# An RWKV block on one core: own sums in the decay product's fourth column tile, a first mix input from PSUM, and a new order

## The chip, the core and the metric

The kernel runs on one core of one Trainium2 chip. The core's engines are TensorE (PE in the profile, with PEld for its weight loads), VectorE (DVE), ScalarE (ACT), GpSimd (POOL) and SyncE (SP, which here only issues loads and stores). The metric is the device time of one execution in microseconds; the time of a version is the median of its runs. Lower is better.

## What is computed

One block of a recurrent network (RWKV) on `x` of shape 8 x 256 x 512 in float32: a normalisation, a mix of each token with the one before it (the token shift), five mixed inputs, a recurrence over the 256 tokens with a 16 x 16 state in each of 32 heads, a normalisation of each head, an output product, and then a second, simpler half. Cut to what matters here:

```python
xn = _ln(x, ln1_w, ln1_b)
sx = _token_shift(xn, state[:, i1])            # previous token minus this one
xxx = jnp.tanh((xn + sx * maa_x) @ maa_w1)     # 5 groups of 32
xxx = jnp.matmul(xxx, maa_w2)
x5 = xn[:, :, None] + sx[:, :, None] * (maa_stack + xxx)
w = jnp.exp(-jnp.exp(time_decay + jnp.tanh(x5[:, :, 1] @ decay_w1) @ decay_w2))
r, k, v = x5[3] @ Wr.T, x5[0] @ Wk.T, x5[2] @ Wv.T
g = silu(x5[4] @ Wg.T)
def step(s, rkvw):                              # over the tokens
    a = k_t[:, :, :, None] * v_t[:, :, None, :]
    out = jnp.einsum('bhk,bhkd->bhd', r_t, u * a + s)
    return (a + w_t[:, :, :, None] * s, out)
x = x + (head_norm(outs) * gn_w + gn_b) * g @ Wo.T
x = x + sigmoid(xr @ ffn_Wr.T) * (square(relu(xk @ ffn_Wk.T)) @ ffn_Wv.T)
```

The term with `u` in a step's output doesn't need the state: it is `v_t` times the sum over a head's 16 channels of `r * u * k`. The kernel computes that sum apart; this document calls it the **own sum** (a token's own part).

## The kernel before, in words

A batch (256 tokens) goes through three stages: `inputs_of_scan` (normalise, mix, the four projections k, v, r, g and the decay w), `scan` (the recurrence) and `rest` (head norm, output product, second half). Stages of neighbouring batches overlap. A class `Plan` collects the pieces of work of every stage, each with its engine, its buffers and a duration. `order` then places them one after another: the numbers in the table `TURNS` are the ranks of the pieces, and the piece of the lowest rank that has its inputs is placed next. The outcome is a fixed instruction order for each engine; each engine works its own list strictly in order.

Arrays lie with channels on the 128 partitions, four blocks of 128 channels in two pairs (q = 0, 1; m = 0, 1 within a pair). TensorE multiplies float32 (two records in the trace for a matmul), either with the whole 128 x 128 array, with four column tiles of 32 side by side ("columns", L400 with 128*32, L794, L872, L930), or with row tiles. PSUM, which TensorE writes, has six tiles `ps` of 2 x 256 columns and one wide tile `wrep`.

The scan of a batch runs in four blocks of 128 channels. For each block come four loads `vs` (v spread over the partitions), on VectorE a multiply by k (L917) and a scan along the tokens (L919, `st`), on GpSimd a multiply by r (L922), and on TensorE the block sum of the four products (L930, 16 matmuls); L936 adds it to `att`. Some of the multiplies by k in the first two batches are GpSimd's (L914).

`att` holds v times the own sum. Before the change `scan` makes it: GpSimd multiplies r by k (L867, `rk`), TensorE sums it over the heads with the head masks `hm`, four matmuls in four column tiles (L872), ScalarE copies the result to `att` in 16 pieces of 32 partitions x 256 (L880), GpSimd multiplies by v (L886).

The decay w takes two small products. The first (L794, "the decay product" below) uses four column tiles at once: two for the 64 columns of `decay_w1` on x5[1], and two for the fifth group of `maa_w1` on the first mix input `xin`, which gives `tb` (L802). That group has only 32 columns; both tiles compute it, so that rows 96 to 127 repeat rows 64 to 95. The second (`w,dw`) follows tanh.

At the launch, batch 0's normalised x is turned by TensorE (L612). Then VectorE makes xn from PSUM (L626, times `ln1_w` plus `ln1_b`), ScalarE makes xn * (1 - maa_x) from it into PSUM (L629, the factor `ow` from L529), and VectorE adds the previous token times maa_x (L655): the first mix input. ScalarE then takes tanh of its product with `maa_w1` (L713, `ta`), TensorE multiplies by `maa_w2` (w2a), and VectorE forms x5 (L748, L751). The head masks `hm` are four small VectorE instructions (L533). The parameter vectors `vec` come by SyncE's queue, the identity `idt` by ScalarE's. Wv is centred on the core: TensorE multiplies it by a matrix, and ScalarE copies the four results (L515).

## Time and profile before

| | |
|---|---|
| median of 3 runs | 609.45 us (609.26 to 609.94) |
| span of the profiled execution, first to last instruction | 607.3 us |
| lies around the span, median less span | 2.15 us |
| TensorE busy | 597.2 us |
| VectorE, ScalarE, GpSimd busy | 543.9, 514.6, 520.2 us |
| TensorE clock granted | 1.000 |
| read from and written to memory | 115.25 and 8.39 MB |

The page gives the span as the profiled execution's own time; what lies around it is known only from the median. A row of a group gives line, engine, operation, output <- inputs, shapes and count, then the busy time and the mean of one in ns, then the idle time ahead of it and what ended it. A row of a timeline gives the start, the length, the engine, the line, the operation and the count; neighbours of one kind are merged. A busy TensorE means only that a matmul was in flight.

### The profile page before, as it was taken

To read this page: it belongs to the slowest core of one execution; us is meant where nothing else is said; L and a number is where in the kernel's file an instruction comes from. 1 tells how busy PE (TensorE), PEld (TensorE's weight loads), DVE (VectorE), ACT (ScalarE), POOL (GpSimd) and SP (SyncE) were. 2 spreads that over 40 slices of the span, in tenths; PEclk is the share of its full clock that TensorE was granted. 3 is DMA by queue.
4 is the path that set the end of the run, shared out by engine and by line. 5 is a ranking of instruction groups with operands and counts; after the bars stand their busy time and mean duration, and the time that the engine had idled before them with its cause. 6 is when DMAs were issued, how large, how long until landed. Compare 5 with 4: busy or idle time off the path is not lost.

```text
span 607.3 us, 17606 instructions
## 1 busy us (share of the span) xinstructions
PE 597.2 (98%) x7270; PEld 344.8 (57%) x7270; DVE 543.9 (90%) x492; ACT 514.6 (85%) x1172; POOL 520.2 (86%) x417
## 2 busy tenths in 40 slices
PE   9999999999999999999999999999999999999997
PEld 7675555467544664377553775455644464446464
DVE  6699999999999998899989999999999999995442
ACT  6878779999999999999999898999989799965450
POOL 2899999999899999899989998999898998898020
PEclk9999999999999999999999999999999999999999
DMA  8798855878778787859767996688659877951542
GB/s 319 224 266 218 232 147 142 227 181 215 220 220 215 219 219 205 213 145 268 198 198 191 277 239 189 186 240 225 188 174 263 203 204 227 258 186 42 175 168 92
DMA packets 52640, 124.77 MB, mean 205 GB/s; under 512 B 5841, under 2 KB 11345, under 8 KB 52561
## 3 DMA queue, kind: packets, MB, share of 16 engines
q1 hardware_dynamic: 48048, 119.39, 71.3%
q10 hardware_dynamic: 4512, 4.26, 2.3%
q8 instruction: 57, 0.93, 0.7%
q14 instruction: 23, 0.18, 0.1%
HBM read 115.25 MB, written 8.39 MB: 204 GB/s over the span
## 4 chain that ended last, share of the span: by engine, by line
PE 78%; POOL 14%; DVE 3%; issue 3%; ACT 1%; DMA 1%; DVEq 0%; POOLq 0%; ACTq 0%
PE ps L400 65%; PE ps L930 8%; POOL st L922 7%; PE ps L612 2%; POOL mix L754 2%; PE ps L794 2%; POOL vs L914 2%; DVE st L919 1%; POOL mix L782 1%; POOL att L886 1%; POOL sx L640 1%; PE ps L956 1%; DMA xt<-in_x 1%; PE ps L872 0%; DVE vs L917 0%
## 5 line engine op out<-in xcount | busy, mean ns | idle before, releaser
L919 DVE TENSOR_TENSOR_SCAN st<-wrep,vs 128x1024 f32<-128x1024 f32 x128 | 288.2, 2277 | 2.9 <-ACT wrep L900 0.8
L922 POOL TENSOR_TENSOR st<-st,r 128x1024 f32<-128x1024 f32 x128 | 254.5, 2005 | 9.3 <-DVE st L919 9.0
L917 DVE TENSOR_TENSOR vs<-vs,ps 128x1024 f32<-128x1024 f32 x122 | 143.7, 1208 | 2.6 <-ACT vs L910 2.4
L400 PE MATMUL ps<-Ws,mix 128*32 128x512 f32 (+3 forms) x872 | 115.2, 586 | 0.1
L400 PEld LDWEIGHTS ps<-Ws,mix 128*32 128x32 f32 (+1 forms) x872 | 37.6, 116 | 63.4 <-issue 56.0
L754 POOL TENSOR_TENSOR mix<-mix,xn 128x512 f32<-128x512 f32 x62 | 66.6, 1098 | 6.9 <-DVE mix L738 5.5
L930 PE MATMUL ps<-st,con 128*32 128x256 f32 x1024 | 62.1, 380 | 0.8 <-POOL st L922 0.7
L400 PE MATMUL ps<-mix,Wv 128*32 128x256 f32 (+1 forms) x832 | 60.5, 380 | 1.6 <-DVE mix L751 0.9
L400 PE MATMUL ps<-mix,Wk 128*32 128x256 f32 (+1 forms) x952 | 59.2, 379 | 0.1
L400 PE MATMUL ps<-mix,Wg 128*32 128x256 f32 (+1 forms) x664 | 58.8, 379 | 0.0
L400 PE MATMUL ps<-mix,Wr 128*32 128x256 f32 (+1 forms) x688 | 58.5, 380 | 0.0
L400 PE MATMUL ps<-mix,Ws 128*32 128x256 f32 (+1 forms) x664 | 57.3, 379 | 0.0
L400 PE MATMUL ps<-Ws,g 128*32 128x512 f32 (+1 forms) x416 | 56.9, 593 | 0.2 <-POOL g L1001 0.2
L736 ACT ACTIVATE ps<-ps,vec 128x256 f32<-128x256 f32 x112 | 47.6, 444 | 3.8 <-PE ps L400 2.3
L880 ACT COPY att<-ps 32x256 f32<-32x256 f32 x128 | 46.6, 364 | 4.4 <-ACT v L825 1.3
L668 POOL TENSOR_TENSOR mix<-mix,xn 128x512 f32<-128x512 f32 x44 | 47.3, 1093 | 3.4 <-ACT mix L666 3.2
L400 PEld LDWEIGHTS ps<-mix,Wv 128*32 128x32 f32 (+1 forms) x832 | 37.7, 116 | 21.2 <-DVE mix L751 1.6
L400 PEld LDWEIGHTS ps<-mix,Ws 128*32 128x32 f32 (+1 forms) x664 | 40.0, 124 | 15.5 <-ACT o L1025 0.5
L400 PEld LDWEIGHTS ps<-mix,Wr 128*32 128x32 f32 (+1 forms) x688 | 39.3, 123 | 16.5 <-issue 1.3
L930 PEld LDWEIGHTS ps<-st,con 128*32 128x32 f32 x1024 | 32.7, 110 | 27.5 <-issue 4.4
L400 PEld LDWEIGHTS ps<-mix,Wg 128*32 128x32 f32 (+1 forms) x664 | 39.9, 124 | 14.8 <-issue 0.7
L400 PEld LDWEIGHTS ps<-mix,Wk 128*32 128x32 f32 (+1 forms) x952 | 35.0, 112 | 22.3 <-issue 2.9
(141 smaller groups left out, 968.1 us busy)
## 6 DMA issues: line engine op xcount, KB each, us to landing
vs<-vo SPq DMA_DIRECT2D x128, 512.0 KB, 5.7
Ws<-in_fk SPq DMA_DIRECT2D x16, 512.0 KB, 6.1
Ws<-in_wo SPq DMA_DIRECT2D x16, 512.0 KB, 6.2
Ws<-in_fr SPq DMA_DIRECT2D x16, 512.0 KB, 6.1
Ws<-in_fv SPq DMA_DIRECT2D x16, 512.0 KB, 5.2
x<-in_x SPq DMA_DIRECT2D x9, 512.0 KB, 8.0
vo<-v ACTq DMA_DIRECT2D x15, 256.0 KB, 5.4
out<-o SPq DMA_DIRECT2D x15, 256.0 KB, 4.9
```

The source lines that it names most:

```text
L400: nc.tensor.matmul(out[i : i + n], lhsT=w[:, i : i + n], rhs=x, start=first, stop=final)
L612: nc.tensor.transpose(to[:, m, n * P : (n + 1) * P], xh[n]()[:, k * P : (k + 1) * P], idt())
L668: gp(512, t, [t, xn[q]], lambda q=q, t=t: nc.gpsimd.tensor_tensor(t(), t(), xn[q]()[:, :, 1 : T + 1], ALU.add))
L736: act(256, p_, [p_, vec], lambda g=g, q=q, m=m, p_=p_: nc.scalar.activation(p_()[:, m, :], p_()[:, m, :], AF.Identity, bias=col(f"maa_{g}" ...
L754: gp(512, t, [t, xn[q]], lambda q=q, t=t: nc.gpsimd.tensor_tensor(t(), t(), xn[q]()[:, :, 1 : T + 1], ALU.add))
L794: nc.tensor.matmul(pd()[i : i + 32, 0, :], lhsT=w, rhs=src[k // 2]()[:, k % 2, :], start=(k == begin), stop=(k == end))
L880: act(350, atts[q], [pc], lambda i=32 * (2 * q + m), m=m, q=q, h=32 * h: nc.scalar.copy(atts[q]()[h : h + 32, m, :], pc()[i : i + 32, 0, :]))
L914: gp(4 * T, vs, [vs, k], lambda m=m, vs=vs, k=k: nc.gpsimd.tensor_tensor(vs(), vs(), k.place[:, m : m + 1, 1 : T + 1].to_broadcast([P, 4, ...
L917: dve(4 * T, [vs], [vs, kp], lambda m=m, vs=vs, kp=kp: nc.vector.tensor_tensor(vs(), vs(), kp()[:, m : m + 1, :].to_broadcast([P, 4, T]), ...
L919: dve(4 * T, [st], [w, vs], lambda w=w, vs=vs, st=st: nc.vector.tensor_tensor_scan(st().rearrange("p n t -> p (n t)"), w().rearrange("p n ...
L922: gp(4 * T, st, [st, r], lambda m=m, st=st, r=r: nc.gpsimd.tensor_tensor(st(), st(), r()[:, m : m + 1, :].to_broadcast([P, 4, T]), ALU.mul ...
L930: nc.tensor.matmul(pat()[32 * i : 32 * i + 32, 0, :], lhsT=con()[:, s : s + 32], rhs=done[i]()[:, j, :], start=(j == 0), stop=(j == 3),)
```

## The change

The own sums of batches 0 to 6 move into the decay product of the next batch: its fourth column tile, rows 96 to 127, no longer repeats the `maa_w1` columns but multiplies one block of `rk` by `hm`. Their results lie in two PSUM tiles, the decay product's own `pd` and one more. `tb` is therefore written in four pieces of 32 partitions, not in two of 64. ScalarE copies the sums to `att` in eight pieces of 32 x 512. Batch 7 keeps the old form. The multiplies `rk` move from `scan` to the end of `inputs_of_scan`, and the stages are put down in a new sequence, with the inputs of batch b + 1 ahead of the scan of b.

At the launch the first mix input comes straight from PSUM: ScalarE makes `xn * (1 - maa_x)` from PSUM with combined factors `ow` and bias `ln1_b`, VectorE adds the previous token from PSUM times `xw`, and the first column has a one-element instruction of its own with `xb`. `ow`, `xw` and `xb` take six small GpSimd instructions in place of one. Of the four centred Wv pieces VectorE copies two. `vec` is loaded by ScalarE's queue. `TURNS` is new throughout.

```diff
+        if b == NB - 1: ...   (batch 7: product and 16 copies as before)
+        else:
+            for q, pc in enumerate(got["pc"]):
+                for h in range(0, P, 32):
+                    act(610, atts[q], [pc], lambda q=q, h=h, pc=pc: nc.scalar.copy(atts[q]()[h : h + 32], pc()[96:128]))
...
-                    for i in range(0, P, 32):
+                    for i in range(0, P if b == 0 else 96, 32):
                         w, src = (dw1()[:, k, i : i + 32], x5[1]) if i < DEC else (w1()[:, k, P + i - DEC : P + i - 32], xin)
                         nc.tensor.matmul(
                             pd()[i : i + 32, 0, :], lhsT=w, rhs=src[k // 2]()[:, k % 2, :], start=(k == begin), stop=(k == end))
+                    if own:
+                        nc.tensor.matmul(own["pc"][k // 2]()[96:128, k % 2, :], lhsT=hm()[:, k, :],
+                                         rhs=own["rks"][k // 2]()[:, k % 2, :], start=True, stop=True)
...
-        for rows in (slice(0, 64), slice(64, 128)):
-            act(T, tb, [pd], lambda rows=rows: nc.scalar.activation(tb()[rows, :], pd()[64:128, 0, :], AF.Tanh), "exp")
+        n = 32 if own else 64
+        for rows in (slice(i, i + n) for i in range(0, P, n)):
+            act(T, tb, [pd], lambda rows=rows: nc.scalar.activation(tb()[rows, :], pd()[64 : 64 + n, 0, :], AF.Tanh), "exp")
...
                 if first:
+                    t = first[q]
+                    a = new(("sq", "o")[m], f"xa_{q}_{m}")
+                    act(256, a, [ps, ow, vec], lambda m=m, k=k, a=a, ps=ps: nc.scalar.activation(
+                        a()[:, 0:T], ps()[:, m, :], AF.Identity, bias=col("ln1_b", k), scale=ow()[:, k : k + 1]), pointers=2)
+                    dve(1, [t], [ps, ow, xb], lambda m=m, k=k, t=t, ps=ps: nc.vector.tensor_scalar(
+                        t()[:, m, 0:1], ps()[:, m, 0:1], ow()[:, k : k + 1], xb()[:, k : k + 1], ALU.mult, ALU.add))
+                    dve(256, [t], [ps, a, xw], lambda m=m, k=k, t=t, a=a, ps=ps: nc.vector.scalar_tensor_tensor(
+                        t()[:, m, 1:T], ps()[:, m, 0 : T - 1], xw()[:, k : k + 1], a()[:, 1:T], ALU.mult, ALU.add), 1.28)
                     dve(256, [xn], [ps, vec], lambda m=m, k=k, xn=xn, ps=ps: nc.vector.tensor_scalar(
                         xn()[:, m, 1 : T + 1], ps()[:, m, :], col("ln1_w", k), col("ln1_b", k), ALU.mult, ALU.add))
-                    t = ps
-                    act(256, t, [xn, ow], lambda m=m, k=k, t=t, xn=xn: nc.scalar.activation(
-                        t()[:, m, :], xn()[:, m, 1 : T + 1], AF.Copy, scale=ow()[:, k : k + 1]), pointers=1)
...
-            act(512, w, [ps], lambda ps=ps, w=w: nc.scalar.copy(w(), ps().rearrange("p m t -> p (m t)")))
+            if k % 2:
+                act(512, w, [ps], lambda ps=ps, w=w: nc.scalar.copy(w(), ps().rearrange("p m t -> p (m t)")))
+            else:
+                dve(512, [w], [ps], lambda ps=ps, w=w: nc.vector.tensor_copy(w(), ps().rearrange("p m t -> p (m t)")))
...
+    plan.add("ACT", 0.4, [vec], [], lambda: nc.scalar.dma_start(out=vec(), in_=vecs), kb=64)
-    load(vec, vecs, 64)
...
     TURNS = """
-        1 69 8 22 53 86 91 104 59 88 92 103 194 171 11 27 85 123 124 180 9 7 10 38 39 63 31 52 68 37 41 44 46 47 48,
+        5 3 49 10 30 35 34 85 67 56 71 61 76 39 4 18 23 13 14 15 25 103 115 118 121 8 7 9 38 62 68 48 72 82 52
```

What this moves is seen in the instruction lists. In them the lines are those of the changed kernel where it is the changed kernel's list (L794 is now L812, the own sums stand at L815, L930 is L962, L533 is L556, L748 and L751 are L766 and L769, L713 is L731). A row gives the line, the operation, output <- inputs with the numbers of the buffers, and the shape of the output.

TensorE before, at batch 0's own sums (about 53 us): two projections' last rows, the own sums of batch 0 by themselves, and the block sum.

```order
L400 MATMUL ps_170<-mix_113,Wg_81 32x256 x8
L400 MATMUL ps_174<-mix_108,Wg_80 32x256 x8
L400 MATMUL ps_174<-mix_113,Wg_81 32x256 x8
L872 MATMUL ps_173<-rk_151,hm 32x256 x2
L872 MATMUL ps_173<-rk_152,hm 32x256 x2
L930 MATMUL ps_171<-st_156,con 32x256
L930 MATMUL ps_171<-st_154,con 32x256
```

TensorE in the changed kernel at the same place: batch 1's decay product with batch 0's own sums in it, between the g projection and the block sum.

```order
L410 MATMUL ps_176<-mix_115,Wg_83 32x256 x8
L812 MATMUL ps_175<-mix_114,dw_69 32x256 x2
L812 MATMUL ps_175<-mix_111,mw_66 32x256
L815 MATMUL ps_175<-rk_153,hm 32x256
L812 MATMUL ps_175<-mix_114,dw_69 32x256 x2
L812 MATMUL ps_175<-mix_111,mw_66 32x256
L815 MATMUL ps_175<-rk_153,hm 32x256
L812 MATMUL ps_175<-mix_113,dw_69 32x256 x2
L812 MATMUL ps_175<-mix_109,mw_66 32x256
L815 MATMUL ps_173<-rk_154,hm 32x256
L962 MATMUL ps_176<-st_158,con 32x256
```

The four separate matmuls are gone; in each group of four column tiles the second copy of `mw` has become a matmul on `rk`, and the decay product, which before came after this block sum, now comes ahead of it.

VectorE before, at the launch between batch 1's statistics and the third x5 input (`mix_111` and `mix_115` are the second and last pieces of x5[2], from which Wv is multiplied).

```order
L574 BN_STATS st_89<-x_161 128x6
L575 BN_AGGR mv_92<-st_89 128x2
L748 SCALAR_TENSOR_TENSOR ps_170<-ps_170,vec,sx_103 128x256 x2
L751 TENSOR_TENSOR mix_111<-ps_170,xn_99 128x512
L748 SCALAR_TENSOR_TENSOR ps_172<-ps_172,vec,sx_104 128x256 x2
L751 TENSOR_TENSOR mix_115<-ps_172,xn_100 128x512
L533 TENSOR_SCALAR hm<-con,vec 128x32
```

VectorE in the changed kernel, the same stretch from the last piece of the first mix input on (`mix_113` and `mix_117` are the pieces of x5[2]).

```order
L651 SCALAR_TENSOR_TENSOR mix_110<-ps_172,xw,o_166 128x255
L528 COPY Wv_79<-ps_177 128x512
L528 COPY Wv_78<-ps_174 128x512
L653 TENSOR_SCALAR xn_102<-ps_172,vec 128x256 x2
L595 BN_STATS st_92<-x_163 128x6
L595 BN_STATS st_91<-x_163 128x6
L596 BN_AGGR mv_94<-st_92 128x2
L596 BN_AGGR mv_94<-st_91 128x2
...
L769 TENSOR_TENSOR mix_113<-ps_174,xn_101 128x512
L766 SCALAR_TENSOR_TENSOR ps_176<-ps_176,vec,sx_106 128x256 x2
L556 TENSOR_SCALAR hm<-con,vec 128x32
L769 TENSOR_TENSOR mix_117<-ps_176,xn_102 128x512
```

Two Wv copies and two xn pieces now stand ahead of the statistics, and a head mask stands ahead of the last addition, where before it came behind it.

ScalarE before, at the very start.

```order
L1058 DMA idt<-in_consts 128x128
L462 ACT_TABLE_LOAD
L462 ACTIVATE mn_94<-eh 128x2
L565 ACTIVATE rs_95<-mv_91,eh 128x1
L565 ACTIVATE rs_96<-mv_92,eh 128x1
```

ScalarE in the changed kernel, at the very start.

```order
L1091 DMA vec<-in_vecs 128x128
L472 ACT_TABLE_LOAD
L472 ACTIVATE mn_96<-eh 128x2
L1090 DMA idt<-in_consts 128x128
L586 ACTIVATE rs_97<-mv_93,eh 128x1
```

The vectors take the identity's place at the head of the queue; the identity is issued behind the table load and the first activation.

77 lines of the change are left out of this document (42 added, 35 removed), and 246 rows, old and new, of the table TURNS.

## The prediction

> **What bounds the kernel now.** I read the page first: the busy time of each engine, then the chain that ended last.
>
> ```profile
> PE 597.2 (98%) x7270; PEld 344.8 (57%) x7270; DVE 543.9 (90%) x492; ACT 514.6 (85%) x1172; POOL 520.2 (86%) x417
> PE 78%; POOL 14%; DVE 3%; issue 3%; ACT 1%; DMA 1%; DVEq 0%; POOLq 0%; ACTq 0%
> ```
>
> TensorE (PE) is busy for 98% of the span and carries 78% of the chain, so work taken from it should shorten the kernel. But GpSimd (POOL) carries 14%, and an average does not say where. The busy times by stretch (columns: length, then PE, PEld, DVE, ACT, POOL) and the chain in order of time do.
>
> ```profile
> 50.00:75.00 25.00, 25.00 (x464) 14.78 (x458) 25.00 (x22) 20.09 (x47) 25.00 (x18) 1.00 0.89 222
> 450.00:500.00 50.00, 50.00 (x724) 26.63 (x720) 48.26 (x43) 44.06 (x100) 46.49 (x36) 1.00 0.83 218
> ...
> 34.21 2.00 POOL st L922
> ...
> 140.21 1.97 POOL st L922
> 142.22 1.93 PE ps L930 x32
> ```
>
> Between 50 and 75 us GpSimd and VectorE never rest either; between 450 and 500 only TensorE is always busy. The chain hangs mostly on GpSimd's multiplies from 34 us up to the block sum at 142 us (L930, TensorE's sum over the four products of one block), and from there on TensorE. TensorE's own timeline has the wait at that point:
>
> ```profile
> 142.22 1.93 PE L930 MATMUL ps<-st,con 128*32 128x256 f32 x32 [0.33 <-POOL st L922]
> ```
>
> So there are three stages: a launch, in which each engine waits for another; a GpSimd stage up to 142 us, in which TensorE work is free; and a TensorE stage, in which it is the price. The sum is made against the span of 607.3; the median of the runs, 609.45, lies 2.15 above it, and I keep that.
>
> **The change, part by part. The own sums.** Seven of the eight products at L872 vanish as work of their own: they go into the fourth column tile of the decay product (L794), which until now computed rows 64 to 95 a second time in rows 96 to 127.
>
> ```profile
> 182.66 0.61 PE L872 MATMUL ps<-rk,hm 128*32 128x256 f32 x8
> 183.09 1.91 PE L400 MATMUL ps<-mix,Wv 128*32 128x256 f32 x32
> ...
> busy tenths in 40 slices 0002002000002020000200000200002000200000
> L872 PE MATMUL ps<-rk,hm x64: 379/379/403, 52.9 to 523.5; 128*32 128x256 f32 x64
> L794 PE MATMUL ps<-mix,mw x128: 379/379/403, 19.3 to 484.2; 128*32 128x256 f32 x128
> ```
>
> One of them costs 183.09 - 182.66 = 0.43 us of TensorE, start to start. The new instructions have the shape of those that they replace (L872 and L794 both 379 ns, the same tile), so the fourth column costs nothing more. The marks of L872 in 40 slices of 15.2 us are at slices 3, 6, 12, 14, 19, 25, 30 and 34: the first two lie before 142 us, where TensorE has time to spare, and the last one, batch 7's, stays. What counts is **5 x 0.43 = 2.15 us off**. If the two early ones counted as well it would be 3.0.
>
> ScalarE copies the sums out in another form:
>
> ```profile
> L880 ACT COPY att<-ps 32x256 f32<-32x256 f32 x128 | 46.6, 364 | 4.4 <-ACT v L825 1.3 <-PE ps L872 1.3
> L825 ACT COPY k<-ps 128x512 f32<-128x512 f32 x16 | 9.3, 581 | 3.1 <-PE ps L400 3.0
> L802 ACT ACTIVATE tb<-ps 64x256 f32<-64x256 f32 x16 | 6.1, 381 | 0.7 <-ACT v L843 0.4
> ```
>
> Sixteen copies at 0.364 are 5.8 us a batch; eight copies of twice the columns, by the nearest row 0.58 each, are 4.6; two more tanh pieces at 0.38 add 0.8. That is 0.4 us less ScalarE work a batch, 2.8 in seven. ScalarE stands on 1% of the chain, so of the bounds, nothing and 2.8 off, I take nothing; TensorE's own work hides it. The products r*k move ahead on GpSimd, sixteen before and after, nothing.
>
> **The launch.** The rows of VectorE, TensorE, ScalarE and GpSimd, by engine:
>
> ```profile
> 7.15 1.00 DVE L626 TENSOR_SCALAR xn<-ps,vec 128x256 f32<-128x256 f32 x2 [0.53 <-PE ps L612]
> 9.39 1.66 DVE L655 SCALAR_TENSOR_TENSOR mix<-xn,vec,ps 128x256 f32<-128x256 f32 x4
> 11.12 0.69 DVE L574 BATCH_NORM_STATS2 st<-x 128x6 f32<-128x512 f32 x1
> 14.35 1.02 DVE L748 SCALAR_TENSOR_TENSOR ps<-ps,vec,sx 128x256 f32<-128x256 f32 x2 [1.51 <-PE ps L400]
> 16.01 1.01 DVE L748 SCALAR_TENSOR_TENSOR ps<-ps,vec,sx 128x256 f32<-128x256 f32 x2
> 17.05 0.69 DVE L751 TENSOR_TENSOR mix<-ps,xn 128x512 f32<-128x512 f32 x1
> 17.66 1.17 DVE L533 TENSOR_SCALAR hm<-con,vec 128x32 f32<-128x32 f32 x1
> ...
> 17.53 1.27 POOL L744 TENSOR_TENSOR mix<-mix,sx 128x512 f32<-128x512 f32 x1
> ...
> 10.52 1.94 PE L400 MATMUL ps<-mix,mw 128*128 128x256 f32 x8
> 17.80 1.13 PE L400 MATMUL ps<-mix,Wv 128*128 128x256 f32 x4
> 26.61 0.71 PE L400 MATMUL ps<-tb,mw2b 32*128 32x256 f32 x8
> ...
> 12.62 0.38 ACT L713 ACTIVATE ta<-ps 128x256 f32<-128x256 f32 x1
> ...
> L567 DVE RECIPROCAL rs<-rs 128x1 f32<-128x1 f32 x2 | 0.3, 155 | 0.0
> ```
>
> Before, VectorE makes four xn pieces and four mix pieces, and the first mix input stands at 9.39 + 1.66 = 11.05. Now only two xn pieces lie ahead: 2 x 0.50, four one-column pieces (at 0.155, the nearest short row) 0.6, and 1.66, from 7.15 to 10.4: 0.65 earlier. TensorE's first product then ends near 12.0 instead of 12.46, and tanh starts about 0.5 earlier than 12.62.
>
> VectorE gives that back. It waited 1.51 us for TensorE ahead of 14.35; now two copies of Wv (0.69 each, by L751's width), two xn pieces (1.0) and batch 1's statistics (two of 0.69 and two short ones of 0.18) follow 10.4: 10.4 + 1.4 + 1.0 + 1.4 + 0.4 = 14.6. The second mix (L748 and L751, twice) so starts 0.25 later, not 0.5 earlier. And one head mask (L533) stands between its last multiply and its last addition. That small instruction took 1.17 us before, from 17.66 to 18.83, and GpSimd's multiply ended at 17.53 + 1.27 = 18.80: it waited for GpSimd. TensorE takes up Wv at 17.80 on what this addition writes.
>
> The Trainium skill, page "SBUF — State Buffer", section "Who interferes with whom", says that a VectorE instruction in a two-port mode, tensor_scalar from SBUF among them, shuts out GpSimd for its whole length or is shut out by it, whichever starts later. This row agrees, and by the rule the mask costs up to a whole GpSimd multiply in its new place.
>
> From the rows alone the mask costs 0.1 (GpSimd idle) to 1.17, so the second x5 input is 0.25 + 0.1 to 0.25 + 1.2 later, 0.4 to 1.4. Against it stands the product from tb (26.61): half of the k projection now comes behind it, which lets the adds that follow it start earlier. For the start of the GpSimd stage I keep -0.6 (the earlier mix alone) to +1.5 and take the middle, **0.5 us later**.
>
> The two small loads change places on ScalarE's queue:
>
> ```profile
> idt<-in_consts ACTq DMA_DIRECT2D x1, 64.0 KB, 3.2
> vec<-in_vecs SPq DMA_DIRECT2D x1, 64.0 KB, 4.9
> ...
> 5.99 1.33 PE L612 MATMUL ps<-idt,xh 128*128 128x128 f32 x8
> 2.45 0.20 ACT L462 ACTIVATE mn<-eh 128x2 f32<-128x2 f32 x1
> ```
>
> The vectors go first and by idt's row land near 0.7 + 3.2 = 3.9; six short GpSimd pieces on them are then done long before 7.15. SyncE's queue loses one issue, and Wg moves ahead of con. But the identity is now issued behind the instruction that ends at 2.65, and lands between 2.65 + 3.2 = 5.9 and 2.65 + 4.9 = 7.6. The transposes want it at 5.99. That is 0 to 1.6 late; I take nothing, since ScalarE's queue showed the 3.2.
>
> The Trainium skill, page "DMA: Bandwidth & Descriptors", section "Issuing engines are not separate DMA queues", says that loads issued from several engines share the same DMA engines and that only issue time is saved. By that the identity would land nearer to 7.6, and the sum would be up to 1.6 higher; no run here shows it yet.
>
> **New turns.** From the block sum at 142 us to the end the TensorE work in program order shrinks by the five sums and nothing else; changes between array shapes are as many, 110 before and after. What the new order does to waits in the TensorE stage cannot be read from it; bounded by the rival below.
>
> The sum: 607.3 - 2.15 + 0.5 = 605.65, with the 2.15 outside the span **607.8 us**.
>
> **The rivals.** *The launch gives it all back.* The mask waits for GpSimd, the identity comes late, and the GpSimd stage, which has no slack, ends 1.5 us later: 609.45 - 2.15 + 1.5 = 608.8, within 0.2% (1.2 us, about what a measurement of this kernel can tell from no change). For it: VectorE's row of work up to 14.6. Against it: idle time at the launch can take up small delays.
>
> *A wait at the decay product (the slower side).* Own sums now exist only when the next batch's decay product has run, so the new order has that product close behind the small products (w2a) that feed it. In batches 4 and 5 sixteen narrow products of 512 columns (32 records of the trace) stand between the two, where three and more times that stood before. These rows price them, the path between the two in batch 2, and what can stand ahead on the way:
>
> ```profile
> L400 PE MATMUL ps<-Ws,mix 128*32 128x512 f32 x800 | 90.3, 593 | 0.0
> L919 DVE TENSOR_TENSOR_SCAN st<-wrep,vs 128x1024 f32<-128x1024 f32 x128 | 288.2, 2277 | 2.9 <-ACT wrep L900 0.8
> L922 POOL TENSOR_TENSOR st<-st,r 128x1024 f32<-128x1024 f32 x128 | 254.5, 2005 | 9.3 <-DVE st L919 9.0
> ...
> 92.20 1.15 PE L400 MATMUL ps<-ta,mw2a 32*128 32x256 f32 x16
> 96.28 1.11 POOL L754 TENSOR_TENSOR mix<-mix,xn 128x512 f32<-128x512 f32 x1
> 98.13 0.41 PE L794 MATMUL ps<-mix,dw 128*32 128x256 f32 x2
> ```
>
> The work between is 32 x 90.3 / 800 = 3.6 us. In batch 2 the products end at 93.35 and GpSimd's addition at 97.39: a path of 4.0, in which another GpSimd piece took 1.1. With that path TensorE waits 0.4 in each of the two batches, and the kernel comes to 608.6. With a scan (2.3) ahead on VectorE and a multiply (2.0) ahead on GpSimd in place of that piece the path is 4.0 - 1.1 + 4.3 = 7.2, the wait 3.6 twice, the time 607.8 + 7.2 = 615.0. Slower than before by over 0.2%, 610.7, begins at a wait of 1.45 a batch, a path of 5.0. For it: VectorE and GpSimd are busy for nine tenths of those stretches. Against it: batch 2 went through with 0.7 to spare (98.13 against 97.39) while both were full.
>
> *All seven sums count,* because the launch also starts 0.6 earlier: 609.45 - 3.0 - 0.6 = 605.85. *The fourth column is not free* (its results go to two PSUM tiles): four instructions of 0.38 in a row instead of side by side cost 7 x 4 x 0.38 = 10.6, 618. The equal rows speak against it.
>
> **How the numbers follow.** Forecast 607.8, 607.0 to 608.6 by itself: 0.42, of which 0.36 below 608.2. Seven sums and launch: 0.10. The launch gives it back: 0.30, of which 0.28 within 0.2% and 0.02 below. The wait: 0.16, of which 0.04 within. The column: 0.02. Faster by over 0.2%: 0.36 + 0.10 + 0.02 = 0.48; within: 0.06 + 0.28 + 0.04 = 0.38; slower: 0.12 + 0.02 = 0.14. The range reaches down to the seven sums and up into the waits, and leaves out some 0.04 below and 0.12 above: 605.6 to 610.6.
>
> **What would show it.** In the profile after: no own sum by itself but batch 7's; the decay product's instructions still 379 ns; the first GpSimd multiply of a block at 34.7 instead of 34.21, and the head mask near 17 us long; the block sum that ended GpSimd's stretch 0.5 later than 142.2; from there to the end 2.15 less. Wrong would be: waits of TensorE at the decay products of batches 4 and 5, transposes later than 6.0, or a GpSimd stage that ends earlier than before.

## The result, and the profile after

The changed kernel is slower: 618.63 us median of 4 runs (617.2 to 620.14) against 609.36 us before (608.96 to 609.94), a ratio of 1.0151 with a 95% interval of 1.0128 to 1.0174. The forecast was 607.8 with a range of 605.6 to 610.6.

The page after, the same two rows as before (busy time by engine, then the chain that ended last):

```profile
PE 597.1 (97%) x7094; PEld 349.6 (57%) x7094; DVE 544.7 (89%) x498; ACT 508.5 (83%) x1128; POOL 520.8 (85%) x422
PE 66%; ACT 13%; DVE 9%; POOL 6%; DMA 3%; issue 3%; ACTq 0%; SPq 0%; DVEq 0%; POOLq 0%
```

TensorE has fewer instructions (7094 instead of 7270) and is busy as long, and its share of the chain fell from 78% to 66%: ScalarE now has 13% where it had 1%. Of the 176 records that are gone, 56 go with the own sums; the other 120 are five projections that the new turns put through the whole array (8 records each) instead of four column tiles (32 records). Either form takes about as long (behind 147 us in the new trace 1.72 and 1.76 us from one to the next). A busy time doesn't show a short wait, so the loss has to be placed by marks that both traces have. Four of them, from the timelines:

| mark, us | before | after | later by |
|---|---|---|---|
| first GpSimd multiply of a block | 34.21 | 37.20 | 2.99 |
| seventh block sum, the end of GpSimd's stretch | 142.22 | 145.24 | 3.02 |
| last (32nd) block sum | 555.16 | 561.59 | 6.43 |
| end of the span | 607.3 | 615.4 | 8.1 |

The profiled run took 617.2 (a span of 615.4 and 1.8 around it), so the table accounts for a run of 617.2. The launch lost 3.0 us, and GpSimd's stretch handed them on unchanged (108.0 us from the first multiply to the seventh block sum in both). The TensorE stage, forecast to be 2.15 shorter, lost 3.4 more, and the end another 1.7. The rest of the median's 9.27 us comes from the two runs of 620.1; the profiled one isn't among them.

The rows of the marks, before (the seventh, at 142.22, stands in the prediction) and after:

```profile
155.47 1.93 PE L930 MATMUL ps<-st,con 128*32 128x256 f32 x32
555.16 1.93 PE L930 MATMUL ps<-st,con 128*32 128x256 f32 x32
...
145.24 1.93 PE L962 MATMUL ps<-st,con 128*32 128x256 f32 x32
156.77 1.93 PE L962 MATMUL ps<-st,con 128*32 128x256 f32 x32
158.52 1.91 PE L410 MATMUL ps<-mix,Ws 128*32 128x256 f32 x32
561.59 1.93 PE L962 MATMUL ps<-st,con 128*32 128x256 f32 x32
```

The eighth block sum comes 13.25 us behind the seventh before and 11.53 after. TensorE is busy all that time in both; the projection at 158.52, one of four that stood ahead of the eighth, now stands behind it. So 1.7 us of work has moved, and a count that starts at the eighth block sum makes the new order look 1.7 us worse than one that starts at the seventh.

The rows that answer to those of the launch before, by engine; ahead of them two of before that the prediction doesn't show:

```profile
3.80 0.69 DVE L563 BATCH_NORM_STATS2 st<-xt 128x6 f32<-128x512 f32 x1 [2.61 <-DMA xt<-in_x]
27.39 1.13 PE L400 MATMUL ps<-w,dw 64*128 64x256 f32 x8
...
4.54 0.69 DVE L584 BATCH_NORM_STATS2 st<-xt 128x6 f32<-128x512 f32 x1 [3.35 <-DMA xt<-in_x]
8.55 0.55 DVE L653 TENSOR_SCALAR xn<-ps,vec 128x256 f32<-128x256 f32 x1 [1.20 <-ACT sq L647]
10.55 0.54 DVE L653 TENSOR_SCALAR xn<-ps,vec 128x256 f32<-128x256 f32 x1 [0.70 <-ACT o L647]
12.50 0.47 DVE L651 SCALAR_TENSOR_TENSOR mix<-ps,xw,o 128x255 f32<-128x255 f32 x1
19.02 1.20 DVE L556 TENSOR_SCALAR hm<-con,vec 128x32 f32<-128x32 f32 x1
20.13 0.68 DVE L769 TENSOR_TENSOR mix<-ps,xn 128x512 f32<-128x512 f32 x1
...
9.50 0.56 ACT L647 ACTIVATE sq<-ps,vec,ow 128x256 f32<-128x256 f32 x1 [0.90 <-DVE mix L649]
11.71 0.56 ACT L647 ACTIVATE o<-ps,vec,ow 128x256 f32<-128x256 f32 x1 [1.19 <-DVE mix L651]
...
6.73 1.33 PE L633 MATMUL ps<-idt,xh 128*128 128x128 f32 x8 [0.77 <-DVE xh L589]
12.12 1.99 PE L410 MATMUL ps<-mix,mw 128*128 128x256 f32 x8 [1.37 <-DVE mix L651]
29.89 1.13 PE L410 MATMUL ps<-w,dw 64*128 64x256 f32 x8
...
37.20 2.00 POOL L954 TENSOR_TENSOR st<-st,r 128x1024 f32<-128x1024 f32 x1
```

Three things are to be seen. VectorE takes up x at 4.54, before at 3.80, and the transposes that follow start at 6.73 instead of 5.99. The first mix input is complete at 12.97, where 10.4 was forecast and 11.05 stood before: VectorE waits for ScalarE and ScalarE for VectorE, in turns, over one and the same PSUM tile that both only read. And the head mask (L556) took 1.20 us ahead of the last addition for Wv. The product from w, from which the scan's decay comes, starts at 29.89 instead of 27.39.

The own sums in the decay product (L812, L815) and their copies (L913), from the views of the lines and of the groups:

```profile
L812 PE MATMUL ps<-mix,dw x128: 377/379/403, 23.7 to 482.6; 128*32 128x256 f32 x128
L815 PE MATMUL ps<-rk,hm x56: 379/379/403, 57.0 to 482.6; 128*32 128x256 f32 x56
...
L913 ACT COPY att<-ps 32x512 f32<-32x512 f32 x56 | 32.4, 579 | 2.1 <-PE ps L815 1.2 <-POOL g L1033 0.2
```

The fourth column is free (379 ns as before; in e9, which has decay products of both kinds in the order of before, the whole of batch 3's takes 1.73 us with own sums where it took 1.72 without), and a copy costs 0.579, as taken (0.58). These steps were right. What TensorE waited for after GpSimd's stretch (columns: total, times, longest), first before, then after:

```profile
PE ps L400 <- DVE o L1050: 0.8, 1, 0.8
PE ps L612 <- DVE xh L582: 0.4, 1, 0.4
...
PE ps L410 <- ACT mix L1048: 1.4, 2, 0.7
PE ps L410 <- DVE mix L678: 0.7, 1, 0.7
PE ps L962 <- DVE mix L756: 0.5, 1, 0.5
PE ps L410 <- DVE mix L756: 0.5, 1, 0.5
```

All rows together are 2.0 us before and 5.0 after. That is the smaller part of the loss: from the seventh block sum to the end TensorE counts as busy for 461.6 us instead of 459.9, though it has about 2 us less to do, so the larger part stands in no row of waits. No row after names a decay product (L812), the place of the rival with the wait. Several of the new waits (on L1048, L756, L851) are for an instruction that reads a PSUM tile out.

### The profile page after: what moved, and what is told of

It reads as the page before. It is cut to its first block, busy times and chain, and to the rows that moved or that the text cites. A ratio compares the mean times of both kernels' runs of the same rounds, so it can differ in the third digit from the quotient of the medians.

```text
span 615.4 us, 17209 instructions
## 1 busy us (share of the span) xinstructions
PE 597.1 (97%) x7094; PEld 349.6 (57%) x7094; DVE 544.7 (89%) x498; ACT 508.5 (83%) x1128; POOL 520.8 (85%) x422
## 4 chain that ended last, share of the span: by engine, by line
PE 66%; ACT 13%; DVE 9%; POOL 6%; DMA 3%; issue 3%; ACTq 0%; SPq 0%; DVEq 0%; POOLq 0%
PE ps L410 55%; PE ps L962 7%; DVE st L951 3%; POOL st L954 3%; DMA vs<-vo 2%; PE ps L633 2%; ACT sq L1021 2%; DVE vs L949 2%; PE ps L812 1%; ACT ps L754 1%; POOL mix L772 1%; ACT rk L1021 1%; ACT wrep L932 1%; ACT att L1028 1%; DVE mix L756 1%
## 5 line engine op out<-in xcount | busy, mean ns | idle before, releaser
L962 PE MATMUL ps<-st,con 128*32 128x256 f32 x1024 | 61.8, 380 | 3.1 <-DVE mix L795 1.6
L962 PEld LDWEIGHTS ps<-st,con 128*32 128x32 f32 x1024 | 33.9, 110 | 30.5 <-issue 8.9
L410 PEld LDWEIGHTS ps<-mix,Wv 128*32 128x32 f32 (+1 forms) x760 | 39.8, 119 | 18.8 <-DVE mix L769 2.4
L410 PEld LDWEIGHTS ps<-mix,Wk 128*32 128x32 f32 (+1 forms) x784 | 38.3, 118 | 18.9 <-POOL mix L772 1.6
L410 PEld LDWEIGHTS ps<-mix,Wr 128*32 128x32 f32 (+1 forms) x808 | 37.3, 117 | 20.0 <-issue 0.9
L754 ACT ACTIVATE ps<-ps,vec 128x256 f32<-128x256 f32 x112 | 45.7, 446 | 1.5 <-PE ps L410 0.4
L664 POOL TENSOR_TENSOR sx<-xn 128x512 f32<-128x512 f32 x30 | 30.9, 1039 | 15.4 <-DVE xn L653 9.0
```

The lines of the kernel that those rows point to most:

```text
L410: nc.tensor.matmul(out[i : i + n], lhsT=w[:, i : i + n], rhs=x, start=first, stop=final)
L664: take(512, [sx], [xn], lambda xn=xn, sx=sx, e=nc.vector if quick else nc.gpsimd: e.tensor_tensor(sx(), xn()[:, :, 0:T], xn()[:, :, 1 : T ...
L754: act(256, p_, [p_, vec], lambda g=g, q=q, m=m, p_=p_: nc.scalar.activation(p_()[:, m, :], p_()[:, m, :], AF.Identity, bias=col(f"maa_{g}" ...
L962: nc.tensor.matmul(pat()[32 * i : 32 * i + 32, 0, :], lhsT=con()[:, s : s + 32], rhs=done[i]()[:, j, :], start=(j == 0), stop=(j == 3),)
```

## The experiments

All times are medians, beside runs of the kernel before on the same chip (609.2 to 609.7). "First multiply" and "sums 8 to 32" (start of the eighth to start of the last block sum) are from the profiled run. Line numbers of these kernels lie up to some ten off those of the changed kernel, as their tables of turns are shorter.

| run | us (lowest to highest) | ratio to before, 95% | first multiply | sums 8 to 32 |
|---|---|---|---|---|
| before | 609.4 | | 34.21 | 399.7 |
| changed | 618.6 (617.2 to 620.1) | 1.0128 to 1.0174 | 37.20 | 404.8 |
| e1 launch of before | 624.1 (623.5 to 625.1) | 1.0223 to 1.0255 | 34.31 | 404.0 |
| e2 launch into before | 618.8 (618.3 to 619.9) | 1.0137 to 1.0168 | 37.36 | 399.6 |
| e3 tiles in turn, first try | 622.9 (616.9 to 624.4) | 1.0146 to 1.0251 | 39.85 | 403.1 |
| e4 own sums early | 654.8 (654.7 to 655.0) | 1.0722 to 1.0758 | 37.86 | 435.4 |
| e5 own sums into before | 689.6 (688.6 to 690.8) | 1.1294 to 1.1335 | 34.56 | 468.7 |
| e6 own sums apart | 627.5 (625.7 to 628.8) | 1.0266 to 1.0320 | 37.17 | 408.5 |
| e7 tiles in turn | 618.2 (616.4 to 619.4) | 1.0118 to 1.0173 | 36.32 | 403.2 |
| e8 identity by SyncE | 618.7 (617.4 to 619.8) | 1.0132 to 1.0168 | 37.22 | 404.9 |
| e9 three sums into before | 620.8 (620.5 to 622.8) | 1.0186 to 1.0214 | 34.48 | 409.4 |
| e10 launch mended | 616.6 (614.4 to 617.5) | 1.0096 to 1.0133 | 36.14 | 404.2 |
| e11 five PSUM tiles | 753.6 (752.9 to 755.5) | 1.2355 to 1.2389 | 41.65 | |
| e12 early release | 627.3 (625.8 to 629.3) | 1.0278 to 1.0317 | 37.33 | 412.4 |
| e13 launch mended further | 618.7 (616.6 to 622.4) | 1.0139 to 1.0200 | 37.22 | 403.4 |
| e14 changed, again | 617.4 (616.9 to 621.0) | 1.0116 to 1.0162 | 37.30 | 406.2 |
| e15 launch operations into before | 609.9 (609.5 to 612.3) | 1.0003 to 1.0021 | 35.29 | 400.0 |
| e16 masks elsewhere in before | 609.2 (608.4 to 609.8) | 0.9984 to 1.0002 | 34.52 | 399.7 |
| e17 halves of x | 618.8 (617.5 to 620.8) | 1.0135 to 1.0180 | 36.53 | 406.9 |
| e18 mended, and halves | 616.4 (614.7 to 616.9) | 1.0091 to 1.0127 | 36.32 | 404.6 |

Two cautions on the last column. Between an old and a new order 1.7 us of it are the projection that has moved. And ten traces have the changed kernel's order behind the launch (changed, e1, e3, e7, e8, e10, e13, e14, e17, e18): with a granted clock of 1.00 throughout that stretch they lie between 403.1 and 406.9, the changed kernel itself at 404.8 and 406.2. The four with the order of before (before, e2, e15, e16) lie between 399.6 and 400.0.

### Launch and later turns exchanged (e1, e2)

```diff
 changed kernel (e1)                      kernel before (e2)
-launch operations as changed            -launch operations as before
+launch operations as before             +launch operations as changed
-turns as changed                        -turns as before
+turns of before up to the first         +turns of the change up to the first
+multiply, those of the change behind    +multiply, those of before behind
```

> The changed kernel with the launch of before: its operations, and its order up to the first multiply of the scan; own sums and all later turns as changed. In the trace after the change the first GpSimd multiply of a block starts at 37.20 instead of 34.21 us, and the block sum that ends GpSimd's stretch at 145.24 instead of 142.22, 3.0 later both times. Theory 1, the launch costs 3.0 us and passes them on unchanged: 618.6 - 3.0 = 615.6, first multiply near 34.2. Rival, the delay is taken up later and all of the loss lies in the TensorE stage: 618.6.

> The kernel before with the launch of the change: its operations, and its order up to the first multiply of the scan; own sums by themselves and all later turns as before. Theory 1, the launch costs 3.0 us: 609.4 + 3.0 = 612.4, block sum that ends GpSimd's stretch near 145.2. Rival, the delay is taken up: 609.4.

Neither number came. At the seam the two orders don't fit, and TensorE stood still there (timelines, first e1, then e2):

```profile
57.40 6.36 PE L405 MATMUL ps<-mix,Wg 128*32 128x256 f32 x64 [4.96 <-DVE mix L744]
...
47.76 5.21 PE L409 MATMUL ps<-mix,Wk 128*32 128x256 f32 x64 [3.82 <-DVE mix L755]
```

The medians therefore say nothing of the launch. What the traces do say lies behind the seam: with the turns of before the sums 8 to 32 take 399.6 with the new launch, with those of the change 404.0 with the old one; less the 1.7 that moved, some 2.7 are lost. The end goes with the turns too: from the last block sum to the end of the span it is 51.8 us in the five experiments with the old turns and six tiles (e2, e5, e9, e15, e16; 52.1 in the trace of before) and 53.5 to 53.9 in every trace with the new ones, with own sums late (changed) or apart (e4, e6). So what is lost behind GpSimd's stretch belongs to the turns and the own sums, not to a late start.

### The own sums (e4, e5, e6, e9)

```diff
 e4: changed kernel
...
-        if b == NB - 1:
+        if True:
...
 with r*k, product, copies, the product with v and the block additions ahead, where before had them

 e5: kernel before, launch and turns kept
+ the change's decay product with own sums, and its eight copies, placed directly behind it

 e6: changed kernel, launch and turns kept
...
-        if b == NB - 1:
+        if True:
...
 with the product directly ahead of the decay product, two copies in each place of one

 e9: as e5, for batches 1, 2 and 5 only
-        own = gots[b - 1] if b else None
+        own = gots[b - 1] if b - 1 in (1, 2, 5) else None
...
```

> The changed kernel, its launch and its turns, but the own sums of every batch by themselves again, as soon as r*k is there; their copies, the product with v and the additions of the block sums stand where the order of before had them among their neighbours. Theory 2, own sums that come only with the next batch's decay product hold the block sums in PSUM (on average 10 us after the change, 8 before) and TensorE waits for tiles: 2.15 of work come back, some 5 us of waits go: 615.8, and TensorE's waits after 145 us fall. Rival, the new order costs the 5 us whatever the own sums do: 618.6 + 2.15 = 620.8.

> The kernel before, its launch and its turns, with only the own sums changed: in the decay product's fourth column tile, copied out in eight pieces behind it. Theory A, the work is saved and nothing waits: five sums of 0.43 us in the TensorE stage, 609.6 - 2.15 = 607.4, decay product still 1.73 us. Theory B, own sums that come later hold the block sums in PSUM and TensorE waits for tiles, so that the change needs new turns: above 609.6, with waits of TensorE after 145 us.

> The changed kernel, its launch and its turns, but each own sum again a product by itself, directly ahead of the decay product that it was in, with its sixteen copies where the eight are now. The term itself: 2.15 (five in the TensorE stage) to 3.0 us (all seven) more than the changed kernel's 618.6, 620.8 to 621.6; if the sums were not on the path that sets the end, 618.6.

> The kernel before, its launch and its turns, with the own sums in the next batch's decay product for batches 1, 2 and 5 alone. In its trace the decay product followed the own sums of these batches by 1.2, 2.1 and 9.1 us, for batches 3 and 4 by 36.4 and 44.7. Theory, what counts is how long the sums have to wait: nothing waits here, and the two sums that lie in the TensorE stage save 0.43 us each, 609.3 - 0.86 = 608.4. Rival, own sums in the column always cost waits: above 609.8.

e6 tries the term that the prediction began with: the new turns, and the own sums by themselves. Its median is 627.5 - 618.6 = 8.9 us longer, far above the 2.15 to 3.0 expected, but most of that isn't the term. In its trace, 11.6 us above that of the changed kernel, 8.2 had arisen by the seventh block sum (153.45 instead of 145.24), where TensorE's clock was at half from 87.9 to 91.3 and from 122.1 to 128.9 us. The sums 8 to 32, all at full clock, took 408.5: 3.7 more than in the changed kernel's first trace, and 1.6 to 5.4 more than in the ten with its order. So the term has the right sign, and 2.15 lies in that range; its size can't be read more closely. The copies were undone with it.

e5 shows why it can't be had alone: in the old turns the same saving costs 80 us. (Its trace has the clock at half for 55 us in all, so this is the waits and the slow work behind them together.) e9 has the mechanism in three rows. It moved batch 5's own sums behind, by the 9.1 us that lay between them and the next decay product (timelines of TensorE, VectorE and GpSimd):

```profile
413.32 6.56 PE L408 MATMUL ps<-mix,Wk 128*32 128x256 f32 x64 [4.57 <-DVE att L959]
...
412.84 0.76 DVE L959 TENSOR_TENSOR att<-ps,att 128x256 f32<-128x256 f32 x2 [4.74 <-POOL att L909]
...
411.72 1.09 POOL L909 TENSOR_TENSOR att<-v,att 128x512 f32<-128x512 f32 x1 [1.89 <-ACT att L904]
```

From the bottom: GpSimd's product with v waits for the copies of the own sums, VectorE's addition of the block sum for GpSimd, and TensorE for the PSUM tile in which that block sum lay. e9 was expected at 608.4 and took 620.8: its sums 8 to 32 are 9.7 us longer, though two sums of 0.43 are saved. Of that 7.7 arose here: TensorE stood still for 4.57 us, and then its clock was at half from 412.4 to 419.3, another 3.4. Most of the rest arose at batch 2's own sums, though they had been moved by only 2.1 us: there TensorE stood still 1.70 us for a copy of the own sums (its wait names L904) and 0.75 for an addition (L959). So in the turns of before a late own sum is paid for by TensorE, in a unit (a tile) that the prediction had not counted.

e4 was to show that the TensorE stage recovers when the sums come early. Its sums of batches 3 and 4 did come 16 and 32 us ahead of the first block sum of their batch, and the stretch grew to 435.4 us (5.1 of them by a halved clock). Copies, products and additions change their places in the queues with them, so it doesn't tell lateness from order and settles nothing beyond this: early sums don't go with the new turns, as late ones don't with the old.

### PSUM tiles (e11, e12)

```diff
 e11: kernel before
-    pool("ps", 6, [P, 2, T], pp)
+    pool("ps", 5, [P, 2, T], pp)

 e12: changed kernel, batches 3, 4 and 6
-                dve(256, [att], [pat, att], ... att()[:, m, :], pat()[:, 0, :], att()[:, m, :], ALU.add
+                if m == 0:
+                    ab = new("mix", f"ab{b}_{q}")
+                dve(256, [ab], [pat], ... tensor_copy(ab()[:, m, :], pat()[:, 0, :])
+                if m == 1:
+                    gp(512, att, [ab, att], ... tensor_tensor(att(), ab(), att(), ALU.add))
```

> The kernel before with five PSUM tiles in its pool instead of six, nothing else. Measures how short of tiles the TensorE stage is. Theory, TensorE waits for tiles that are read out late: several us more than 609.4, with waits of TensorE after 145 us where there were 1.0 us. Rival, tiles are plenty: 609.4.

> The changed kernel, in which VectorE, in batches 3, 4 and 6, copies each block sum out of PSUM at once into a free tile, and GpSimd adds the pair to the product with the own sums when that is there; before, the block sum stayed in PSUM until then (up to 31.6 us). GpSimd gets two additions of 1.09 us a batch more. Theory, tiles held by block sums that wait for late own sums cost TensorE its 5 us after GpSimd's stretch: 1 to 3 us less than the changed kernel, the stretch from the eighth block sum to the last shorter than its 404.8. Rival, the order itself costs it: 404.8 and 618.6, or more for the added work.

One tile less costs the kernel before 144 us; VectorE's and GpSimd's instruction lists are the same in it, and its clock is at half for 78 us, so that waits and slow work are again together. The waits of TensorE in e11, after 145 us, two of the rows:

```profile
PE ps L400 <- DVE mix L738: 19.8, 10, 3.0
PE ps L400 <- DVE att L936: 12.2, 7, 5.6
```

L936 is the addition that frees a block sum's tile; before the change its row in this view read 0.2. So this stage has no tile to spare. But e12 went against its theory: freeing them at once made the stretch 412.4 us instead of 404.8. VectorE's copy now stands right behind the block sum in its queue and waits for it (6.1 us in three waits between 244 and 310 us), and GpSimd has the additions besides. That holding tiles costs TensorE time is shown in e9 and e11, in the turns of before; how much of what the changed kernel loses behind GpSimd's stretch it makes up, and how much is the order as such, stays open.

### The launch (e3, e7, e8, e10, e13, e15, e16, e17, e18)

VectorE's and ScalarE's order over the two PSUM tiles of the first mix (A and B), rows of e3 and e7 against the changed kernel's; sq and o are ScalarE's four passes:

```diff
 VectorE  changed: xn B | first columns A, B | mix B | xn B | mix B, A, A
+e3: xn A, xn A | mix B, B | mix A, A | xn B, xn B       (ScalarE: sq B, o B, sq A, o A)
+e7: the same, with ScalarE's copy of xn's first column for A ahead of sq B
```

> The changed kernel with another order at the launch, nothing else: ScalarE takes both passes over one PSUM tile while VectorE works on the other, then they change places. In the trace after the change VectorE waits for ScalarE three times (1.20, 0.70 and 0.24 us) and ScalarE for VectorE twice (0.90 and 1.19) between 7.9 and 13.0 us, always on a tile that the other engine reads. Theory, two readers of one PSUM tile take turns and the handing over costs: the first mix input is complete at about 11.5 to 11.8 instead of 12.97, and the kernel 0.8 to 1.4 shorter: 617.2 to 617.8. Rival, the waits have another cause: 12.97 and 618.6.

> The changed kernel with another order at the launch: VectorE's xn pieces on one PSUM tile while ScalarE passes over the other, then they change places once. In the first try of it (e3) the second pass of ScalarE over the tile was ahead of VectorE's pieces, so VectorE began at 9.58 us, the mix was complete at 13.6, and TensorE, which had stood still for 2.97 us, ran at a clock of 0.50 from 15 to 18.3. Theory, readers of one tile take turns: mix complete at 11.6 to 11.9 instead of 12.97, no stretch at half clock at the launch, first multiply of a block 0.8 to 1.3 earlier than 37.20, median 617.2 less that: 616.0 to 616.6. Rival: 618.6.

In e3 one wait was left, and it was the wrong one: VectorE began only behind ScalarE's pass over tile A. Its rows of TensorE and of the clock (windows of 1 us; the third column from the end is the granted clock):

```profile
13.67 2.52 PE L407 MATMUL ps<-mix,mw 128*128 128x256 f32 x8 [2.97 <-DVE mix L648]
...
14.00:15.00 1.00, 1.00 (x6) 0.90 (x5) 1.00 (x3) 0.97 (x1) 0.33 (x1) 1.00 1.05 405
15.00:16.00 1.00, 1.00 (x5) 0.74 (x4) 1.00 (x3) 0.00 (x0) 1.00 (x2) 0.50 1.04 406
```

In e7 no engine waits for the other between 8.3 and 11.6 us, the mix is complete at 11.66, and the first multiply starts at 36.32 instead of 37.20:

```profile
8.26 1.00 DVE L650 TENSOR_SCALAR xn<-ps,vec 128x256 f32<-128x256 f32 x2 [0.75 <-PE ps L630]
...
36.32 2.00 POOL L951 TENSOR_TENSOR st<-st,r 128x1024 f32<-128x1024 f32 x1
```

That is the 0.8 to 1.3 expected there. The median gained only 0.4 (618.2): three of the four runs had a lowered clock, and the one without took 616.4. The Trainium skill, page "PSUM — Partial Sum Buffer", section "PSUM bank collisions raise a hardware error", says that any two engines on one bank and quadrant collide, two readers included, and must be kept apart by semaphores. The trace agrees in so far as the readers of one tile took turns and the cost went when each engine had a tile to itself; a collision no run shows.

```diff
 e8: changed kernel
-    plan.add("ACT", 0.4, [idt], [], lambda: nc.scalar.dma_start(out=idt(), in_=consts[:, 0:P]), kb=64)
+    load(idt, consts[:, 0:P], 64)     (SyncE, behind the two halves of x)

 e10: changed kernel, order only
+ as e7; identity ahead of the vectors; last product for Wv behind the first w2a product;
+ head mask behind the last addition for Wv

 e13: e10, order only
+ all of k's product ahead of the one from tb, its copies behind it; all masks where VectorE waits for tb

 e17: changed kernel, order only          e18: e10, with the same
-load x, second half                     -load x, second half
 load x, first half                       load x, first half
+load x, second half                     +load x, second half
```

> The changed kernel with the identity issued by SyncE right behind the two halves of x, instead of by ScalarE behind the vectors; the vectors stay at the head of ScalarE's queue. In the four traces so far with both small loads on ScalarE VectorE took up x at 4.49 to 4.72 us, in the two with the identity alone there at 3.80 and 3.89. Theory, the second small load ahead of x costs this: x at 3.8 to 3.9, and the kernel 0.7 shorter than the changed one. Rival, it is the vectors themselves: 4.5 to 4.7, no change.

> The changed kernel with four pieces of its launch in another order and nothing else: the vectors behind the identity on ScalarE's queue; VectorE and ScalarE on different PSUM tiles as in e7; the last product for Wv behind the first small products; the head mask behind the last addition for Wv. By the traces these cost 0.7 (x taken up at 4.54 instead of 3.80), 0.9 (e7), 0.6 (15.18 - 14.53, before 0.05) and 1.0 (second mix input 3.08 later, the first 2.09). Theory, the launch's loss is the sum of such pieces: x at 3.8 to 3.9, first multiply of a block 34.0 to 35.0 instead of 37.20, block sum that ends GpSimd's stretch as much earlier, 617.2 - 2.7 = 614.5 where TensorE keeps its clock, 616.2 to 617.4 where it loses it once in that stretch. Rival, the pieces hide each other: first multiply above 36, 617 to 618.6.

> The changed kernel with e10's four changes of order and two more: the whole k product ahead of the one from tb, with its copies behind it, as before the change; all head masks where VectorE waits for tb. In e10 x was still taken up at 4.58, tb's product started at 26.27 (before the change 26.61), but k's product ended at 28.8 and the first scan started at 33.25 instead of 31.85, since half of k stood behind tb. Theory, that half is the larger part of what is left of the launch's loss: first scan 31.9 to 32.5, first multiply 34.3 to 35.2 instead of 36.14, kernel 0.9 to 1.8 below e10's 616.6. Rival, the launch's loss does not lie in k: 36.1 and 616.6.

> The changed kernel with the two loads of batch 0's x in the order of before: the half that VectorE takes first is loaded first. The new turns had put the other half ahead of it. VectorE took up x at 4.49 to 4.80 us in every run with the new turns at the launch, at 3.62 to 4.06 in every run with the old ones, e15 among them, which has the vectors and the identity on ScalarE's queue as the change has. Theory, the swapped halves cost x 0.7 us: x at 3.7 to 3.9, first multiply 36.4 to 36.8 instead of 37.2 to 37.3, 0.4 to 0.8 less than 617.2 where TensorE keeps its clock. Rival, the two small loads on ScalarE's queue delay x: 4.5 to 4.7, no change.

> e10 (four pieces of the launch in another order) with the halves of x put right as well. Theory, the pieces add up: first multiply 35.4 to 35.8 instead of e10's 36.14 and the changed kernel's 37.2 to 37.3, and 613.6 to 614.0 where TensorE keeps its clock (e10: 614.4 and 616.1). Block sums eight to thirty-two stay at some 404 us, so that the kernel stays 4 us or more above before: what is left is the TensorE stage. Rival, the mended launch is hidden by something that the first multiply waits for otherwise: 36.1.

e8 and e10 let the theory of the small loads fall: x came at 4.55 and 4.58 all the same. The cause was one that reads alike in a list of instructions: the new turns load the second half of x first, and VectorE takes the first. With the halves put right x stands at 3.67 (e17), and the first multiply comes 0.7 earlier than in the two traces of the changed kernel (37.20, 37.30). The median didn't follow (618.8): all four runs had a lowered clock.

```profile
3.67 0.69 DVE L581 BATCH_NORM_STATS2 st<-xt 128x6 f32<-128x512 f32 x1 [2.49 <-DMA xt<-in_x]
...
36.53 2.00 POOL L951 TENSOR_TENSOR st<-st,r 128x1024 f32<-128x1024 f32 x1
```

In e18 the pieces didn't add up (36.32, e10 had 36.14): x came at 3.84, but TensorE's opening products, which run on nothing but zeros until x is there, ended only at 7.43 in that run. Of the launch's 3.0 us, then, the halves are worth 0.7 and the tile in turns 0.9, each tried by itself. The mask and the order of Wv's products brought 0.2 more in e10, where 34.0 to 35.0 had been expected for the first multiply; no run won back more than e10's 1.1. k's product behind tb was a miss: e13 put it right, k was copied at 27.64 instead of e10's 29.81, and the first multiply was 37.22. But e13 moved the head masks too, and beside GpSimd's instructions there the four took 4.3 us (e10: 1.7), so k's order wasn't tried by itself. The remaining 1.2 or so weren't taken apart.

```diff
 e15: kernel before, its turns kept
-launch operations as before
+launch operations as changed, each where the one that it replaces stood

 e16: kernel before, order only
-head masks at 17.66, 20.06 (two) and 31.35 us
+head masks behind the x5 inputs, ahead of what comes from tb
```

> The kernel before with the launch operations of the change (first mix from PSUM, two copies of Wv on VectorE, the vectors by ScalarE's queue), each where the order of before has the operation that it replaces; own sums and all turns as before. In e2, where the order of the launch was the change's too, block sums eight to thirty-two took 399.6 us, as before the change (399.7). Theory 1, the operations alone cost by x (0.7 later) and by PSUM tiles read in turns: first multiply 35.0 to 36.0, the stretch of 399.7 unchanged, 610.2 to 611.5. Rival, they cost nothing in a good order: 609.3.

> The kernel before with its four head masks where VectorE waits for tb (23.3 to 27.35 us) instead of 17.66, 20.06 and 31.35; nothing else. They took 1.17, 0.65 each and 0.58 us there, and GpSimd stood still for 0.90 us before 22.22 for what VectorE had to make next. Theory, GpSimd's stretch passes every gain at the launch on: 0.5 to 1.4 us less than 609.3, 607.9 to 608.8, which would beat both kernels. Rival, the masks hold GpSimd up wherever they stand: 609.3.

e15 is the answer to the launch: the new operations in the old order cost 0.43 us (609.93 against 609.50, interval 0.2 to 1.3), sums 8 to 32 unchanged. In its trace the first multiply is 1.1 later than before, but 0.85 of that stood already at the first transpose (6.84 instead of 5.99), behind TensorE's opening products, which ended at 7.00 in that run instead of 5.87 and are the same in both kernels. So most of the launch's 3.0 us is a matter of its turns, not of its operations. e16 found nothing to gain: 609.18, interval 0.9984 to 1.0002, the rival's number.

### The clock behind the waits (e14)

> The changed kernel itself, to see how its times of 617.2 and 620.1 divide and where a run of the second kind loses 2.9 us. Theory, TensorE's clock is halved once for 3.4 us behind a wait late in GpSimd's stretch, as e7 and e10 showed at 117 to 123 us: where the profiled run has a granted clock below 1, the rows of 117 to 125 show it, and the block sums behind are up to 2 us later. Rival, a halved clock elsewhere, or none.

The kernel is the changed one, without an edit. Four runs took 616.9 to 617.8, one 621.0, and that one was profiled. It had a lowered clock, but so had the run of 617.8 and one of the two of 617.2 in the result: a lowered clock doesn't make every run long. TensorE's rows about the fifth block sum, and the clock, of this run; then those of the first run of the same kernel:

```profile
117.00 0.71 PE L410 MATMUL ps<-tb,mw2b 32*128 32x256 f32 x8 [0.86 <-ACT k L851]
119.36 3.56 PE L962 MATMUL ps<-st,con 128*32 128x256 f32 x32 [1.65 <-DVE mix L795]
...
120.00:121.00 1.00, 1.00 (x14) 0.45 (x8) 0.71 (x2) 0.82 (x3) 1.00 (x2) 0.50 0.98 242
121.00:122.00 1.00, 1.00 (x16) 0.56 (x12) 0.90 (x3) 0.96 (x3) 1.00 (x1) 0.50 1.01 238
...
116.07 0.71 PE L410 MATMUL ps<-tb,mw2b 32*128 32x256 f32 x8 [0.88 <-ACT k L851]
118.43 1.93 PE L962 MATMUL ps<-st,con 128*32 128x256 f32 x32 [1.65 <-DVE mix L795]
...
120.00:121.00 1.00, 1.00 (x16) 0.41 (x12) 0.90 (x3) 0.96 (x3) 1.00 (x1) 1.00 1.09 258
```

The waits are the same in both, 0.9 and 1.65 us a short product apart. In the one run the clock went to half behind them, from 119.4 to 122.7, and one block sum took 3.56 us instead of 1.93; in the other it didn't. By the seventh block sum the one was 2.4 us behind the other. The kernel before waits 0.51 us at this place, and none of its runs showed a clock below 0.999. The Trainium skill, page "TensorE: Matmul & The Clock Gate", section "What's actually happening", gives the half clock as the state after at least one idle window of about 3.4 us, and says that the window runs free of the program. The length seen here agrees, and so does it that the same waits were followed by a half clock in one run and not in another. The idle time doesn't: TensorE stood still for only 0.9 and 1.65 us here, with a product of 0.71 us between, and the measurement decides.

## Why the prediction was wrong

**The step that failed is "New turns".** It said that the TensorE work shrinks "by the five sums and nothing else" and that what the new order does to waits "cannot be read from it", and then entered it at nothing, with a rival of one place as its bound. The order was the largest term. From the seventh block sum to the last the kernel before takes 412.9 us. The new turns with own sums late but apart (e6) take 420.1, 7.1 more. With the own sums in the fourth column they take 416.4, so 3.7 of it are given back: 3.4 lost where 2.15 were to be won. The new turns lost another 1.7 at the end. "Nothing else" was not quite so either: four projections behind 142 us changed from column tiles to the whole array, at about the same time each. Which waits of the new order make up the loss stays open.

**Own sums, 2.15 us.** The mechanism and the free column were right; the size is 3.7 between two single traces, 1.6 to 5.4 against all with the same order, so 2.15 isn't refuted. What was missing is what they cost: a sum that comes with the next batch's decay product comes late, the block sum lies in PSUM until then, and six tiles leave no room, as e5, e9 and e11 show for the turns of before. ScalarE's saved copies were entered at nothing. e6 undid them together with the products, so what they are worth by themselves wasn't measured.

**Launch, 0.5 us later, bounds -0.6 to 1.5.** It was 3.0. "GpSimd's stretch has no slack" was right: the loss went through it whole. The row "the first mix input at 10.4" fell by 2.6 us: 0.7 since x came later (the halves, whose swap the lists quoted ahead of the prediction don't show), and 1.3 since the sum let VectorE's pieces run one behind the other, while ScalarE read the same tile (12.97, and 11.66 in e7). The mask did wait for GpSimd, 1.20 us (forecast 0.1 to 1.17), as the prediction's row and the page that it cites have it.

**Identity 0 to 1.6 late, taken as 0.** It wasn't late, by a reason of its own: the queue issued it at 1.23 us, while the table was being loaded, and not behind the instruction that ends at 2.65:

```profile
1.23 0.38 ACTq L1090 DMA_DIRECT2D idt<-in_consts  x1
idt<-in_consts ACTq DMA_DIRECT2D x1, 64.0 KB, 3.5
```

At 4.7 it was there, with 2.0 to spare. The page's rule on issuing engines, by which it would have come nearer to 7.6, decided nothing here.

**"Half of the k projection behind tb lets the adds start earlier"** was given as a reason against a loss. The product from tb started 0.7 us later than before, not earlier. Putting k's order back (e13) brought nothing, but with the masks moved in the same run that doesn't clear it.

**The rivals.** The slower side was given 0.14, 0.12 of it to a wait at the decay products of batches 4 and 5. No wait came there. The reason behind it, own sums that need the next decay product, points the right way; in e9 its bill came elsewhere, at TensorE's next PSUM tile. The range ended 6.6 us short of the run at full clock and 8 short of the median. The half clock was in no rival; the runs of 620.1 and 621.0 are 2.9 and 3.8 us longer than the one at full clock, and one of 617.2 with a lowered clock isn't longer at all.

No kernel here beat both. The best with the new turns is e18 (616.4), and e16 can't be told from the kernel before.

## What to carry to other kernels

A change that makes a result come later is priced by what waits for that result and by what it holds meanwhile: count the tiles, not only the instructions. Where a new order comes with a change, its cost can be tried apart from the work: the same work in the new order, and the new work in the old one, at a seam that both orders have. An order list that leaves out which half, which tile or which buffer an instruction touches can hide a swap worth more than the edit.
